# Moving the transposed quarter of a two-dimensional Haar transform from the forward to the inverse side of a long convolution kernel

## The chip, the core and the metric

The kernel runs on one core of one Trainium2 chip. The metric is the device time of one execution in microseconds (us); smaller is better. TensorE is called PE here, VectorE DVE, ScalarE ACT, GpSimd POOL and SyncE SP.

## What is computed

The input `x` is (4, 64, 256, 256) f32: four images in each of 64 channels. Four layers follow one another. Layers 0, 2 and 3 are long convolutions, whose filters come from a small sine network and factor into a filter over rows times one over columns for each channel:

```python
k = einsum('ijk,imk->ijmk', hx, hy)      # hx, hy: (256, 64), from the network
y = irfft2(rfft2(x, (512, 512)) * rfft2(k, (512, 512)) / 512)[:256, :256]
out = y + x * bias
```

Layer 1 works in the two-dimensional Haar domain (H rows and W columns, 8 levels each) and mixes channels, in P = 2 paths:

```python
f1 = haar2d(x)
for i in range(2):
    f3 = v[i] * f1
    f4 = einsum('bchw,oc->bohw', f3, conv_w[i])
    acc += sign(f4) * relu(abs(f4) - tau[i])
out = haar2d(acc, inverse=True) + x
```

(with the scales of the levels moved into `v`, `tau` and per-row factors, and with the last addition done as `+ f1` in the Haar domain).

## The kernel before

A convolution over one axis is a product with a 256x256 Toeplitz matrix. An image is two blocks of 128 partitions by 256 columns, the Toeplitz matrix has a triangular zero block, and so one axis of one image costs two matmuls of 256 and two of 128 columns (`toeplitz`, L228). The output comes out transposed, so that rows and then columns give the image back. One Haar direction is done along the free axis by GpSimd, level by level with additions and subtractions (`forward_free` L235, `inverse_free` L257). The other lies across partitions and takes TensorE: either 128x128 matmuls with a Haar matrix, or transposes into PSUM and the levels on another engine.

The four images of a channel are split into two groups (batches 0-1 and 2-3). A **round** handles M = 4 images: two channels of one group. Each group has 32 rounds in each of the phases A and C.

- **Phase A** (L295): the first convolution (`rows` L309, `columns` L316), then the Haar transform (`forward_free`, `product` L333), and a store of the coefficients to DRAM (`coef`, L427). A round is 12 pieces: four rows, four columns, four products of the round before. ACT copies the rows' result out of PSUM (L314); DVE adds the bias term and writes the columns' result (L325); ACT scales the product into `f` (L354).
- **Phase B** (L472): 64 steps of two units for each group: load all channels at some coefficient rows, mix the channels on PE (`mix`, L508), multiply by `v` on DVE (L512), sign and magnitude on ACT (L516, L519), subtract `tau` and threshold on DVE (L523, L526), add on POOL (L531, L534), and store to `mixed` (L547). A unit is three pieces; two PSUM tiles `f4` are in turn.
- **Phase C** (L580): load `mixed`, undo the free direction on POOL (L273, L275), undo the other, then the layers 2 and 3, each as rows and columns, and store `out`. A round of group 0 is 20 pieces, four of them `product` (L613); a round of group 1 is 16, and its inverse transform is done by transposes (`transposes` L624) with the levels on DVE (`inverse_halves` L642), in two halves q of two images each.

All engine orders are written out by hand. The stages lie, in time, as: A of group 0 alone, with the filter network of layers 2 and 3, the spreading of filters over DRAM and the scaling of `tau` interleaved as side pieces (`rest`, L191 to L195); A of group 1 beside B of group 0; C of group 0 beside B of group 1; C of group 1 alone. `beside` (L776) spreads the side pieces evenly over the main pieces. What evacuates PSUM is put off by `later` (L282) and issued at the start of the next piece by `flush`. PSUM tiles of phases A and C come from one pool of four banks (`bank`, L98), used in turn, so the bank of a piece is wanted again four pieces later. All DMAs are issued by SP in program order.

In phase A of group 0, rounds 0 to 29 (`paired`, L300) use matmuls for two of the four images. The other two go by eight transposes (`transposes`, L356), four scalings on ACT (L371, L372), and 17 DVE steps (`forward_psum`, L377), spread two to a piece over the next round; there the store of the round waits for piece 8 instead of piece 6 (L449 to L453). To make this possible the W coefficients stand in the same permuted order as the H coefficients: two halves of 128, each a Haar set of its own but for the coarsest pair. That pair is combined in `coarsest` (L418) for one direction and, for the other, in phase B's `store` when row 0 is stored (L539 to L546), with the two-column constant `first`. Phase C's `product` then is two independent 128-point inverse transforms per image: four 128x128 matmuls with `haarW`, and one ACT copy of 128x512 (L622).

Of the kernel before, what the change touches and what calls it, by code (L numbers as in the profile page):

```python
# [39 lines left out]
P = 128  # L41
# [12 lines left out]
M = CI * NB  # L54
# [15 lines left out]
def conv_haar_kernel(  # L70
    ctx: ExitStack, tc: tile.TileContext, x, zT, w1, wbd, cols, decay, bias, haarW, haarH, ident, wcol, wrow, mixT, first, v, tau, out
# [41 lines left out]
    tp = pool("t", 1, early)  # L113
    tps = pool("tps", 1, early, space=PSUM)
# [89 lines left out]
    wcol_sb = const.tile([P, 6], F32, tag="wcol", name="wcol_sb")  # L204
# [5 lines left out]

    first_sb = const.tile([P, 2], F32, tag="first", name="first_sb")
    nc.sync.dma_start(first_sb, first)
# [22 lines left out]
    def forward_free(src, dst, name):  # L235


        cur, half = src, HALF
        split = lambda t: t.rearrange("p n (h m) -> p n h m", h=2)
        while half >= 1:  # L240
            pair = cur.rearrange("p n (t q) -> p n t q", q=2)
            even, odd = pair[:, :, :, 0], pair[:, :, :, 1]
            if half == 1:
                nc.gpsimd.tensor_tensor(dst[:, :, 0:1], even, odd, ALU.add)
                yield
                nc.gpsimd.tensor_tensor(dst[:, :, HALF : HALF + 1], even, odd, ALU.subtract)
            else:
                m = half // 2
                at = dst.rearrange("p n (h q) -> p n h q", h=2)[:, :, :, m : 2 * m]
                nc.gpsimd.tensor_tensor(at, split(even), split(odd), ALU.subtract)  # L250
                yield
                cur = ac.tile([P, 2 * M, half], F32, tag=f"h{half}", name=f"{name}{half}", bufs=1)
                nc.gpsimd.tensor_tensor(cur, even, odd, ALU.add)
            yield
            half //= 2

    def inverse_free(src, dst, name):  # L257

# [27 lines left out]
    def flush():  # L286
        for op in waiting:
            op()
        waiting.clear()
# [5 lines left out]
    def phase_a():  # L295
# [3 lines left out]

        paired = ROUNDS - 2  # L300
# [32 lines left out]
        def product(t, j):  # L333
# [4 lines left out]
            if t < paired and j >= 2:  # L338
                if j == 2:
                    transposes(t)  # L340
                return
# [14 lines left out]
        def transposes(t):  # L356
            s = st[t]
            ps = tps.tile([P, 4, N], F32, tag="ps", name=f"tps_{t}")
            for e in range(2):
                for m in range(2):  # L360
                    for k in range(2):
                        data = s["fw"][:, 2 * (2 + e) + k, bass.ts(m, P)]
                        nc.tensor.transpose(ps[:, 2 * e + m, bass.ts(k, P)], data, ident_sb)
            odds = tp.tile([P, 4, HALF], F32, tag="odds", name=f"odds_{t}")
            pair = ps.rearrange("p n (t q) -> p n t q", q=2)

            def scale():
                for m in range(2):
                    by = wcol_sb[:, 4 + m : 5 + m]
                    every = pair.rearrange("p (e m) t q -> p e m t q", m=2)[:, :, m]  # L370
                    nc.scalar.activation(odds.rearrange("p (e m) t -> p e m t", m=2)[:, :, m], every[:, :, :, 1], AF.Copy, scale=by)  # L371
                    nc.scalar.activation(every[:, :, :, 0], every[:, :, :, 0], AF.Copy, scale=by)  # L372

            later(scale)
            s["pair"] = forward_psum(pair, odds, s["f"][:, 4:8], f"t{t}_")

        def forward_psum(pair, odds, dst, name):  # L377

            halves = dst.rearrange("p n (h q) -> p n h q", h=2)
            split = lambda t: t.rearrange("p n (h m) -> p n h m", h=2)
            even = pair[:, :, :, 0]
            d = halves[:, :, :, 64:128]
            nc.vector.tensor_tensor(d, split(even), split(odds), ALU.subtract)
            yield

            even2 = pair[:, :, :64, 1]
            odd2 = tp.tile([P, 4, 64], F32, tag="odd2", name=f"{name}odd")
            for q, o in enumerate((even2, odd2)):  # L390
                ds = d.rearrange("p n h (t q) -> p n h t q", q=2)[:, :, :, :, q]
                es = even.rearrange("p n (h t q) -> p n h t q", h=2, q=2)[:, :, :, :, q]
                nc.vector.scalar_tensor_tensor(split(o), ds, -0.5, es, ALU.mult, ALU.add)
                yield
            d = halves[:, :, :, 32:64]
            nc.vector.tensor_tensor(d, split(even2), split(odd2), ALU.subtract)
            yield
            cur = tp.tile([P, 4, 64], F32, tag="h64", name=f"{name}64")
            nc.vector.scalar_tensor_tensor(split(cur), d, -0.5, split(even2), ALU.mult, ALU.add)
            yield  # L400
            half = 32
            while half > 1:
                m = half // 2
                both = cur.rearrange("p n (t q) -> p n t q", q=2)
                d = halves[:, :, :, m : 2 * m]
                nc.vector.tensor_tensor(d, split(both[:, :, :, 0]), split(both[:, :, :, 1]), ALU.subtract)
                yield
                cur = tp.tile([P, 4, half], F32, tag=f"h{half}", name=f"{name}{half}")
                nc.vector.scalar_tensor_tensor(split(cur), d, -0.5, split(both[:, :, :, 0]), ALU.mult, ALU.add)
                yield  # L410
                half = m
            even, odd = cur[:, :, 0:1], cur[:, :, 1:2]
            nc.vector.tensor_tensor(dst[:, :, 0:1], even, odd, ALU.add)
            yield
            nc.vector.tensor_tensor(dst[:, :, HALF : HALF + 1], even, odd, ALU.subtract)
            yield

        def coarsest(t):  # L418

            by_product = 4 if t < paired else 2 * M  # L420
            pairs = st[t]["f"][:, :by_product].rearrange("p n (h q) -> p n h q", h=2)[:, :, :, 0]
            sd = ac.tile([P, 2 * M, 2], F32, tag="sd", name=f"sd_{t}", bufs=2)[:, :by_product]
            nc.gpsimd.tensor_tensor(sd[:, :, 0], pairs[:, :, 0], pairs[:, :, 1], ALU.add)
            nc.gpsimd.tensor_tensor(sd[:, :, 1], pairs[:, :, 0], pairs[:, :, 1], ALU.subtract)
            nc.gpsimd.tensor_copy(pairs, sd)
# [8 lines left out]
        def piece(t, j):  # L434
# [10 lines left out]
            elif j < 2 * M:  # L445
# [3 lines left out]
                if j == M + 2 and t > 1 + paired:  # L449
                    store(t - 2)  # L450
            else:
                if j == 2 * M and 1 < t <= 1 + paired:
                    store(t - 2)  # L453
# [4 lines left out]
            if j == 3 * M - 1 and 0 < t <= paired:  # L458
                run(st[t - 1]["pair"], 2)
            if j < 2 * M and 1 < t <= 1 + paired:  # L460
                run(st[t - 2]["pair"], 2)
# [10 lines left out]
    def phase_b(grp):  # L472
# [63 lines left out]
        def store(s):  # L536
            r0 = s * ROWS
            gt = st[s]["g"]
            if r0 == 0:  # L539

                top, low = (gt[:, 0].rearrange("p b (h k) -> p b h k", h=2)[:, :, h, :] for h in range(2))
                d = bp.tile([P, NB, N], F32, tag="sd", name=f"sd_{grp}", bufs=1)
                one, sign_ = first_sb[:, 0:1], first_sb[:, 1:2]
                nc.vector.tensor_scalar(d, top, one, None, ALU.mult)
                nc.vector.scalar_tensor_tensor(top, low, one, top, ALU.mult, ALU.add)
                nc.vector.scalar_tensor_tensor(low, low, sign_, d, ALU.mult, ALU.add)  # L546
# [33 lines left out]
    def phase_c():  # L580
# [32 lines left out]
        def product(t, n):  # L613
            s = st[t]
            ps = bank(f"c1ps{n}_{t}")
            for m in range(2):
                for h in range(2):
                    nc.tensor.matmul(  # L618
                        ps[:, m, bass.ts(h, P)], s["ci"][:, 2 * n + h, bass.ts(m, P)], haarW_sb, start=True, stop=True
                    )  # L620
            y = s["y", n] = image("t0", f"cz{n}_{t}")
            later(lambda: nc.scalar.copy(y, ps))  # L622

        def transposes(t, q):  # L624
# [15 lines left out]
            s["wops", q] = inverse_halves(ps, z, f"w{q}_{t}_")  # L640

        def inverse_halves(ps, dst, name):  # L642
            src = ps.rearrange("p n h q -> p (n h) q")
            cur, half = wp.tile([P, 8, 1], F32, tag="w1", name=f"{name}1", bufs=2), 1
            nc.vector.tensor_copy(cur, src[:, :, 0:1])
            yield
            while half < P:
                if half < P // 2:
                    o = wp.tile([P, 8, 2 * half], F32, tag=f"w{2 * half}", name=f"{name}{2 * half}", bufs=2)
                else:  # L650
                    o = dst.rearrange("p n (h q) -> p (n h) q", h=2)
# [49 lines left out]
        def piece(t, j):  # L701
# [25 lines left out]
            else:  # L727
# [10 lines left out]
                if j >= M + 8:  # L738
                    turn(alone, 1, 2)

        def piece_alone(t, j):
# [14 lines left out]
            if 3 <= j < 11:  # L756
                turn(t + 1, 0, 2)
            if j >= 8:
# [153 lines left out]
```

## Time and profile before

| what | us |
|---|---|
| median of 4 runs | 2961.3 (2953.39 to 2961.41) |
| profiled execution | 2957.78 |
| its span | 2956.0 |
| group-0 phase A | from about 35 to 498 |
| A of group 1 beside B of group 0 | to about 1200 |
| C of group 0 beside B of group 1 | to about 2210 |
| C of group 1 alone | to the end |

The profile's first part gives the busy time of each engine. Stages are told apart with a view that cuts the span into windows and gives, for each, the busy time of each engine, the granted TensorE clock and the DMA share. In a timeline, rows are: start, length, engine, line, operation, `output<-inputs`, shapes, count, and in brackets the idle time of the engine before the row, with what ended it. f32 matmuls are recorded as two instructions, transposes as one. The length of a PE row overlaps that of the next, so the pace of PE is read from starts.

### The profile page before, as it was taken

The page shows a single profiled execution, that of the slowest core. Times are in us where ns is not written, and L with a number is a line of the kernel's source. Part 1 is how long each engine was busy: PE and PEld are TensorE (multiplying, and loading weights), DVE is VectorE, ACT ScalarE, POOL GpSimd, SP SyncE. Part 2 cuts the span into 40 slices and gives each one's busy share as a digit, 9 for nine tenths or more (in the row PEclk, how much of TensorE's full clock was granted, in tenths as well). Part 3 has the DMA queues.
Part 4 walks back from the last instruction along what each step waited for, and adds up shares of the span by engine and source line. Part 5 has one row for each costly group of instructions (what it writes and reads, how often), then busy time and mean ns, then how long its engine had stood idle before and what let it go on. Part 6 is the DMA issues. An engine that isn't in the chain of part 4 may idle for free.

```text
span 2956.0 us, 47128 instructions
## 1 busy us (share of the span) xinstructions
PE 2865.5 (97%) x16680; PEld 2443.7 (83%) x16680; DVE 1873.9 (63%) x3065; ACT 1164.6 (39%) x1731; POOL 1967.6 (67%) x2500
## 2 busy tenths in 40 slices
PE   5999998999999999899999999999999999999999
PEld 5988998677777777878888888888899999999998
DVE  3666653788778887276666666666636655565555
ACT  1434443555555555344444444444432121212121
POOL 2766776788888888666666666766685445544550
PEclk9999999999999999999999999999999999999999
DMA  7956997898999997676686677667654454445442
GB/s 162 238 170 189 238 237 228 288 334 300 338 329 318 322 328 244 215 262 235 223 280 233 230 256 254 240 226 274 207 161 132 132 148 145 133 133 151 141 132 79
DMA packets 372145, 656.79 MB, mean 222 GB/s; under 512 B 33798, under 2 KB 273319, under 8 KB 371912
## 3 DMA queue, kind: packets, MB, share of 16 engines
q1 hardware_dynamic: 371912, 653.79, 69.0%
q8 instruction: 134, 2.20, 0.3%
q14 instruction: 99, 0.81, 0.1%
HBM read 438.24 MB, written 215.42 MB: 221 GB/s over the span
## 4 chain that ended last, share of the span: by engine, by line
PE 78%; DVE 6%; POOL 3%; issue 2%; DMA 2%; ACT 1%; SPq 0%; POOLq 0%; DVEq 0%; ACTq 0%
PE f L508 13%; PE c1c L232 8%; PE c2r L232 7%; PE c1r L232 7%; PE c2c L232 7%; PE a1ps L232 4%; PE c1c L233 4%; PE c2r L233 4%; PE c1r L233 4%; PE a2ps L232 4%; PE c2c L233 4%; PE c1ps L618 4%; PE a3ps L345 2%; PE a1ps L233 2%; DVE f L512 2%
## 5 line engine op out<-in xcount | busy, mean ns | idle before, releaser
L508 PE MATMUL f<-ft,mix_sb 128*128 128x512 f32 x1024 | 492.0, 603 | 30.0 <-DVE m L526 25.1
L516 ACT ACTIVATE m<-f 128x1024 f32<-128x1024 f32 x256 | 262.4, 1025 | 648.3 <-DVE f L512 623.2
L523 DVE TENSOR_TENSOR f<-f,tau 128x1024 f32<-128x1024 f32 x256 | 315.0, 1230 | 213.9 <-ACT f L519 213.9
L531 POOL TENSOR_TENSOR m<-m,ft 128x1024 f32<-128x1024 f32 x128 | 301.8, 2358 | 189.8 <-DVE m L526 189.3
L534 POOL TENSOR_TENSOR gt<-m,m 128x1024 f32<-128x1024 f32 x128 | 302.6, 2364 | 177.5 <-DVE m L526 117.0
L512 DVE TENSOR_TENSOR f<-f,v 128x1024 f32<-128x1024 f32 x256 | 314.5, 1229 | 111.1 <-PE f L508 109.4
L232 PE MATMUL a1ps<-toep,x 128*128 128x256 f32 x1024 | 307.7, 383 | 16.7 <-DMA toep<-filt 16.7
L232 PE MATMUL a2ps<-toep,ay 128*128 128x256 f32 x1024 | 310.4, 385 | 11.0 <-ACT ay L314 11.0
L526 DVE SCALAR_TENSOR_TENSOR m<-f,m 128x1024 f32<-128x1024 f32 x256 | 311.0, 1215 | 0.1
L508 PEld LDWEIGHTS f<-ft,mix_sb 128*128 128x128 f32 x1024 | 175.6, 191 | 163.3 <-issue 123.5
L232 PE MATMUL c2r<-toep,cy 128*128 128x256 f32 x1024 | 305.8, 380 | 0.0
L232 PE MATMUL c1c<-toep,ch 128*128 128x256 f32 x1024 | 305.8, 380 | 0.0
L232 PE MATMUL c2c<-toep,ch 128*128 128x256 f32 x1024 | 305.8, 380 | 0.0
L670 ACT COPY ch<-c2r 128x512 f32<-128x512 f32 x256 | 148.5, 588 | 381.7 <-PE c2r L233 381.5
L670 ACT COPY ch<-c1r 128x512 f32<-128x512 f32 x256 | 149.5, 590 | 333.6 <-PE c1r L233 332.7
L684 DVE SCALAR_TENSOR_TENSOR o<-cy,bias_sb,c2c 128x512 f32<-128x512 f32 x256 | 188.4, 742 | 144.8 <-PE c2c L233 144.7
L519 ACT ACTIVATE f<-f 128x1024 f32<-128x1024 f32 x256 | 263.5, 1029 | 0.0
L325 DVE SCALAR_TENSOR_TENSOR x<-x,bias_sb,a2ps 128x512 f32<-128x512 f32 x256 | 188.1, 743 | 102.4 <-PE a2ps L233 57.8
L250 POOL TENSOR_TENSOR fw<-x 128x1024 f32<-128x1024 f32 x64 | 121.2, 1894 | 161.0 <-DVE x L325 161.0
L273 POOL TENSOR_TENSOR i<-i,g 128x16 f32<-128x16 f32 (+5 forms) x384 | 208.8, 544 | 27.2
L273 POOL TENSOR_TENSOR i<-g 128x8 f32<-128x8 f32 x64 | 14.2, 222 | 315.0 <-DMA g<-mixed 315.0
L354 ACT ACTIVATE f<-a3ps,wcol_sb 128x512 f32<-128x512 f32 x196 | 131.3, 685 | 226.9 <-PE a3ps L345 139.7
(87 smaller groups left out, 6472.9 us busy)
## 6 DMA issues: line engine op xcount, KB each, us to landing
toep<-filt SPq DMA_DIRECT2D x768, 128.0 KB, 3.4
x<-in_x SPq DMA_DIRECT2D x256, 256.0 KB, 6.1
coef<-f SPq DMA_DIRECT2D x128, 512.0 KB, 4.8
ft<-coef SPq DMA_DIRECT2D x128, 512.0 KB, 7.1
v<-in_v SPq DMA_DIRECT2D x128, 512.0 KB, 7.2
tau<-taus SPq DMA_DIRECT2D x128, 512.0 KB, 7.0
mixed<-gt SPq DMA_DIRECT2D x128, 512.0 KB, 5.9
g<-mixed SPq DMA_DIRECT2D x128, 512.0 KB, 5.5
```

Of the source, the lines that this page charges most:

```text
L232: nc.tensor.matmul(ps[:, m, :], data[:, 0, cut], t[:, which, :], start=True, stop=False)
L233: nc.tensor.matmul(ps[:, m, HALF:], data[:, 1, cut], t[:, which, :HALF], start=False, stop=True)
L273: nc.gpsimd.tensor_tensor(even, s, d, ALU.add)
L508: nc.tensor.matmul(un[u]["f4"][:, j, :], mix_sb[:, u % 2, :], f[:, j, :], start=True, stop=True)
L512: nc.vector.tensor_tensor(f4, f4, weights(st[u // 2]["v"], u % 2), ALU.mult)
L516: nc.scalar.activation(un[u]["m"], un[u]["f4"], AF.Sign)
L519: nc.scalar.activation(un[u]["f4"], un[u]["f4"], AF.Abs)
L523: nc.vector.tensor_tensor(f4, f4, weights(st[u // 2]["tau"], u % 2), ALU.subtract)
L526: nc.vector.scalar_tensor_tensor(un[u]["m"], un[u]["f4"], 0.0, un[u]["m"], ALU.max, ALU.mult)
L531: nc.gpsimd.tensor_tensor(m0, m0, data(st[s]["f"]), ALU.add)
L534: nc.gpsimd.tensor_tensor(data(st[s]["g"]), m0, un[2 * s + 1]["m"], ALU.add)
L670: later(lambda: nc.scalar.copy(y, ps))
```

## The change

The transposes go out of phase A and into phase C's product, and the W coefficients return to natural order.

- Phase A of group 0: all rounds use matmuls for all four images, as rounds 30 and 31 and group 1 did. `transposes`, `forward_psum` and their pools are gone; every store stands at piece 6.
- `forward_free` writes each level's differences as one contiguous run, and phase B's `store` has no repair of row 0; `first` is gone. The constants for `v`, `tau` and the per-row scales follow the natural order.
- Phase C of group 0: per image, the coarse 128 coefficients take two matmuls with `haarW`, the finest 128 two transposes with the identity. ACT copies the coarse half out of PSUM (128x256) one piece later, and another piece later two DVE operations form the last level into `cz`, reading the transposed half in PSUM.
- Phase C of group 1: the levels on DVE run over one chain of 256 instead of two of 128 side by side, 17 steps instead of 15 for each half q, and may start the second half one piece earlier and end the first one piece later.
- `flush` empties its list before it runs it, so that an operation may put off another.

```diff
     def forward_free(src, dst, name):
...
-                m = half // 2
-                at = dst.rearrange("p n (h q) -> p n h q", h=2)[:, :, :, m : 2 * m]
-                nc.gpsimd.tensor_tensor(at, split(even), split(odd), ALU.subtract)
-                yield
+            nc.gpsimd.tensor_tensor(dst[:, :, half : 2 * half], even, odd, ALU.subtract)
+            yield
+            cur = dst[:, :, 0:1]
+            if half > 1:
                 cur = ac.tile([P, 2 * M, half], F32, tag=f"h{half}", name=f"{name}{half}", bufs=1)
-                nc.gpsimd.tensor_tensor(cur, even, odd, ALU.add)
+            nc.gpsimd.tensor_tensor(cur, even, odd, ALU.add)
...
-            if t < paired and j >= 2:
-                if j == 2:
-                    transposes(t)
-                return
             ps = bank(f"a3ps{j}_{t}")
...
-                if j == M + 2 and t > 1 + paired:
+                if j == M + 2 and t > 1:
                     store(t - 2)
             else:
-                if j == 2 * M and 1 < t <= 1 + paired:
-                    store(t - 2)
...
-            if j == 3 * M - 1 and 0 < t <= paired:
-                run(st[t - 1]["pair"], 2)
-            if j < 2 * M and 1 < t <= 1 + paired:
-                run(st[t - 2]["pair"], 2)
...
         def store(s):
-            if r0 == 0:
-
-                top, low = (gt[:, 0].rearrange("p b (h k) -> p b h k", h=2)[:, :, h, :] for h in range(2))
-                d = bp.tile([P, NB, N], F32, tag="sd", name=f"sd_{grp}", bufs=1)
-                one, sign_ = first_sb[:, 0:1], first_sb[:, 1:2]
-                nc.vector.tensor_scalar(d, top, one, None, ALU.mult)
-                nc.vector.scalar_tensor_tensor(top, low, one, top, ALU.mult, ALU.add)
-                nc.vector.scalar_tensor_tensor(low, low, sign_, d, ALU.mult, ALU.add)
...
         def product(t, n):
             s = st[t]
-            ps = bank(f"c1ps{n}_{t}")
+
+            ps = bank(f"c1ps{n}_{t}").rearrange("p w (m q) -> p w m q", m=2)
             for m in range(2):
-                for h in range(2):
-                    nc.tensor.matmul(
-                        ps[:, m, bass.ts(h, P)], s["ci"][:, 2 * n + h, bass.ts(m, P)], haarW_sb, start=True, stop=True
-                    )
+                cut = bass.ts(m, P)
+                nc.tensor.matmul(ps[:, 0, m], s["ci"][:, 2 * n, cut], haarW_sb, start=True, stop=True)
+                nc.tensor.transpose(ps[:, 1, m], s["ci"][:, 2 * n + 1, cut], ident_sb)
             y = s["y", n] = image("t0", f"cz{n}_{t}")
-            later(lambda: nc.scalar.copy(y, ps))
+            half = ac.tile([P, 2, P], F32, tag="half", name=f"half{n}_{t}", bufs=2)
+            pair = y.rearrange("p m (t q) -> p m t q", q=2)
+
+            def finest():
+                nc.vector.tensor_tensor(pair[:, :, :, 0], ps[:, 1], half, ALU.add)
+                nc.vector.tensor_tensor(pair[:, :, :, 1], half, ps[:, 1], ALU.subtract)
+
+            later(lambda: (nc.scalar.copy(half, ps[:, 0]), later(finest)))
...
-            while half < P:
-                if half < P // 2:
-                    o = wp.tile([P, 8, 2 * half], F32, tag=f"w{2 * half}", name=f"{name}{2 * half}", bufs=2)
-                else:
-                    o = dst.rearrange("p n (h q) -> p (n h) q", h=2)
+            while half < N:
+                o = dst
+                if half < HALF:
+                    o = wp.tile([P, 4, 2 * half], F32, tag=f"w{2 * half}", name=f"{name}{2 * half}", bufs=2)
...
-            if 3 <= j < 11:
+            if 3 <= j < 12:
                 turn(t + 1, 0, 2)
-            if j >= 8:
+            if j >= 7:
                 turn(t + 1, 1, 2)
```

More of the change, by code (lines that the diff above doesn't have):

```diff
@@ L70, in conv_haar_kernel @@
 def conv_haar_kernel(
-    ctx: ExitStack, tc: tile.TileContext, x, zT, w1, wbd, cols, decay, bias, haarW, haarH, ident, wcol, wrow, mixT, first, v, tau, out
+    ctx: ExitStack, tc: tile.TileContext, x, zT, w1, wbd, cols, decay, bias, haarW, haarH, ident, wcol, wrow, mixT, v, tau, out
 ):
@@ L112, in conv_haar_kernel @@
     mps = early.enter_context(tc.tile_pool(name="mlp_ps", bufs=2, space=PSUM))
-    tp = pool("t", 1, early)
-    tps = pool("tps", 1, early, space=PSUM)
     def constant(name, src, shape):
@@ L202, in conv_haar_kernel @@
     nc.sync.dma_start(haarH_sb, haarH)
-    wcol_sb = const.tile([P, 6], F32, tag="wcol", name="wcol_sb")
+    wcol_sb = const.tile([P, 4], F32, tag="wcol", name="wcol_sb")
     nc.sync.dma_start(wcol_sb, wcol)
@@ L209, in conv_haar_kernel @@
     nc.sync.dma_start(mix_sb, mixT)
-    first_sb = const.tile([P, 2], F32, tag="first", name="first_sb")
-    nc.sync.dma_start(first_sb, first)
     def load_toeplitz(l, t, bufs):
@@ L238, in forward_free @@
         cur, half = src, HALF
-        split = lambda t: t.rearrange("p n (h m) -> p n h m", h=2)
         while half >= 1:
@@ L242, in forward_free @@
             even, odd = pair[:, :, :, 0], pair[:, :, :, 1]
-            if half == 1:
-                nc.gpsimd.tensor_tensor(dst[:, :, 0:1], even, odd, ALU.add)
-                yield
-                nc.gpsimd.tensor_tensor(dst[:, :, HALF : HALF + 1], even, odd, ALU.subtract)
-            else:
-                m = half // 2
-                at = dst.rearrange("p n (h q) -> p n h q", h=2)[:, :, :, m : 2 * m]
-                nc.gpsimd.tensor_tensor(at, split(even), split(odd), ALU.subtract)
-                yield
+            nc.gpsimd.tensor_tensor(dst[:, :, half : 2 * half], even, odd, ALU.subtract)
+            yield
+            cur = dst[:, :, 0:1]
+            if half > 1:
                 cur = ac.tile([P, 2 * M, half], F32, tag=f"h{half}", name=f"{name}{half}", bufs=1)
-                nc.gpsimd.tensor_tensor(cur, even, odd, ALU.add)
+            nc.gpsimd.tensor_tensor(cur, even, odd, ALU.add)
             yield
@@ L286, in flush @@
     def flush():
-        for op in waiting:
+        ops = list(waiting)
+        waiting.clear()
+        for op in ops:
             op()
-        waiting.clear()
     def run(ops, count):
@@ L298, in phase_a @@
         total = GROUPS * ROUNDS
-        paired = ROUNDS - 2
         st = [dict() for _ in range(total + 1)]
@@ L354, in product @@
             later(lambda: nc.scalar.activation(dst, ps, AF.Copy, scale=wcol_sb[:, m : m + 1]))
[L356 to L416, printed above, removed]
@@ L418, in coarsest @@
         def coarsest(t):
-            by_product = 4 if t < paired else 2 * M
-            pairs = st[t]["f"][:, :by_product].rearrange("p n (h q) -> p n h q", h=2)[:, :, :, 0]
-            sd = ac.tile([P, 2 * M, 2], F32, tag="sd", name=f"sd_{t}", bufs=2)[:, :by_product]
+            pairs = st[t]["f"].rearrange("p n (h q) -> p n h q", h=2)[:, :, :, 0]
+            sd = ac.tile([P, 2 * M, 2], F32, tag="sd", name=f"sd_{t}", bufs=2)
             nc.gpsimd.tensor_tensor(sd[:, :, 0], pairs[:, :, 0], pairs[:, :, 1], ALU.add)
@@ L639, in transposes, with inverse_psum @@
                 s["y", 2 * q + e] = z[:, 2 * e : 2 * e + 2]
[L640 to L644, printed above, removed]
+            s["wops", q] = inverse_psum(ps.rearrange("p n h q -> p n (h q)"), z, f"w{q}_{t}_")
+        def inverse_psum(src, dst, name):
+            cur, half = wp.tile([P, 4, 1], F32, tag="w1", name=f"{name}1", bufs=2), 1
             nc.vector.tensor_copy(cur, src[:, :, 0:1])
             yield
-            while half < P:
-                if half < P // 2:
-                    o = wp.tile([P, 8, 2 * half], F32, tag=f"w{2 * half}", name=f"{name}{2 * half}", bufs=2)
-                else:
-                    o = dst.rearrange("p n (h q) -> p (n h) q", h=2)
+            while half < N:
+                o = dst
+                if half < HALF:
+                    o = wp.tile([P, 4, 2 * half], F32, tag=f"w{2 * half}", name=f"{name}{2 * half}", bufs=2)
                 pair = o.rearrange("p n (t q) -> p n t q", q=2)
@@ L737, in piece @@
                     turn(alone, 0, 2)
-                if j >= M + 8:
+                if j >= M + 7:
                     turn(alone, 1, 2)
@@ L853 @@
     w = np.abs(full).max(axis=1)
-    v, tau = (
-        a[f"L1_conv_{n}"].reshape(2, N, N).transpose(0, 2, 1)[:, order][:, :, order] for n in ("v", "tau")
-    )
+    v, tau = (a[f"L1_conv_{n}"].reshape(2, N, N).transpose(0, 2, 1)[:, :, order] for n in ("v", "tau"))
     by_row = lambda t: f(t.reshape(2, 2, P, N).transpose(2, 0, 1, 3))
@@ L866 @@
         mix[:, g, :, :, g] = a["L1_conv_conv_w"].transpose(2, 0, 1)
-    odd = np.arange(P) % 2
     arrays = {
@@ L894 @@
         "ident": np.eye(P, dtype=np.float32),
-        "wcol": f(np.concatenate([(w**2)[order].reshape(2, P).T, w[order].reshape(2, P).T, (w**2)[order].reshape(2, P).T / 2], axis=1).astype(np.float32)),
+        "wcol": f(np.concatenate([(w**2).reshape(2, P).T, w.reshape(2, P).T], axis=1).astype(np.float32)),
         "wrow": f(w[order].astype(np.float32)),
         "mixT": f(mix.reshape(P, 2, P)),
-        "first": f(np.stack([1.0 - odd, 2.0 * odd - 1.0], axis=1).astype(np.float32)),
         "v": by_row(v),
```

## The prediction

> **What bounds the kernel now.** I read the busy table of the page first, then stages cut by the windows view, then single instructions in the timeline.
>
> ```profile
> PE 2865.5 (97%) x16680; PEld 2443.7 (83%) x16680; DVE 1873.9 (63%) x3065; ACT 1164.6 (39%) x1731; POOL 1967.6 (67%) x2500
> ```
>
> TensorE (PE) is the bound. The windows view (start:end, length, busy time of PE, PEld, DVE, ACT, POOL, granted clock, DMA share, GB/s) shows where it is gapless:
>
> ```profile
> 264.00:449.00 185.00, 185.00 (x1242) 173.34 (x1242) 113.38 (x297) 76.43 (x140) 141.10 (x266) 1.00 0.93 240
> 900.00:1100.00 200.00, 193.80 (x978) 145.48 (x979) 160.32 (x153) 114.16 (x149) 178.46 (x207) 1.00 0.93 318
> 1345.00:1990.00 645.00, 645.00 (x3570) 526.86 (x3569) 426.52 (x430) 298.06 (x422) 435.32 (x409) 1.00 0.71 245
> 2210.00:2900.00 690.00, 690.00 (x4378) 640.09 (x4378) 404.26 (x1157) 141.96 (x243) 341.20 (x481) 1.00 0.47 137
> ```
>
> Row 1 is phase A of group 0 (call it A0), row 3 phase C of group 0 beside phase B of group 1 (C0), row 4 the last phase C (C1): PE never idle, clock full. Row 2, A of group 1 beside B of group 0, has VectorE (DVE) 80% busy and PE 3% idle. So a change in A0 or C0 is worth its PE time, plus the idle gaps it opens or closes.
>
> **PE in A0: +27.3 us.** Timeline of one A0 round, PE rows (start, length, line, operation, count):
>
> ```profile
> 277.61 1.95 PE L345 MATMUL a3ps<-haarH_sb,fw 128*128 128x128 f32 x16
> 279.40 1.04 PE L363 MATMUL tps<-ident_sb,fw 128*128 128x128 f32 x8
> 280.27 0.60 PE L232 MATMUL a1ps<-toep,x 128*128 128x256 f32 x2
> ```
>
> Starts tell the pace, since lengths overlap. An f32 matmul is two instructions, and 16 of them take 279.40-277.61 = 1.79, so 0.224 per matmul; a transpose is one instruction, and eight take 0.87, so 0.109 each. Thirty rounds get 8 matmuls for 8 transposes: 8 x 0.115 = 0.91 a round. The period confirms it: 13.14 us with transposes (264.47, 277.61, 290.75), 14.05 with the full product (a3ps at 1170.77, 1184.82, 1198.87). 30 x 0.91 = +27.3.
>
> **PE in C0: -29.3 us.** Each of 128 images has four L618 matmuls (32 passes in 3.57 us, 0.223 a matmul); two become transposes: 256 x 0.1145 = -29.3. Here the two kinds alternate, which the trace never shows. Between blocks of them (279.40, 280.27) no gap is seen, so I take none; the bound above is 0.11 on each of the 256, as if a transpose cost a matmul (+29).
>
> The Trainium skill, TensorE: Matmul & The Clock Gate, Part 4, speaks against this: transposes do not count as activity for the clock gate, so a stretch of them may fall to half rate. This trace disagrees at this density: rows 1 and 4 hold 8 per 13 us and 16 per 25 us at clock 1.00. By the page, a halved clock for one product stretch of 2.7 us in each of 32 rounds would be an estimated +85 us.
>
> **The W order: -7 us.** Natural order drops the first-row repair in phase B's store (L544-L546, twice). DVE and PE rows of the timeline, first time:
>
> ```profile
> 543.34 1.56 DVE L544 TENSOR_SCALAR sd<-gt,first_sb 128x512 f32<-128x512 f32 x1
> 544.93 2.72 DVE L545 SCALAR_TENSOR_TENSOR gt<-gt,first_sb 128x512 f32<-128x512 f32 x1
> 547.69 1.41 DVE L546 SCALAR_TENSOR_TENSOR gt<-gt,first_sb,sd 128x512 f32<-128x512 f32 x1
> 552.55 3.38 PE L508 MATMUL f<-ft,mix_sb 128*128 128x512 f32 x4 [3.58 <-DVE m L526]
> ```
>
> The threshold of the next unit stands behind them; PE idles 3.58, then runs the four passes in 3.38 where 1.72 is usual: 5.2 lost. The second time (1271-1284) it idles 1.1 twice and loses 0.6: 2.8. Total 8; I take -7, since DVE may be late by itself (0 to -12, all of the DVE work removed). On GpSimd (POOL) the permuted write goes: L250 (permuted) 1894 ns, L253 (plain) 1893: nothing.
>
> **A0's DVE and queues: -12 us.** The 17 DVE steps per round and four scalings on ScalarE (ACT, 2 x (473+448) = 1.84) go; two more L354 come (2 x 0.685 = 1.37). ACT and DVE were not the bound, but DVE holds up PE at two places.
>
> (a) The filter network's three layers sit in rounds of 18.86, 19.89 and 21.21 instead of 13.14: 20.5 extra, of which 3 x 0.87 is their own matmuls; 17.9 is waiting (11.0 idle, the rest slow clock). Its sine waits in ACT's queue for DVE's chain, and phase A's copies stand behind it:
>
> ```profile
> 195.98 0.70 PE L232 MATMUL a2ps<-toep,ay 128*128 128x256 f32 x2 [3.96 <-ACT ay L314]
> ```
>
> The chain (4.6 us) started 1.2 and some 2 us late behind pair steps in two layers, 0.2 in the third. About 3.5 of 11.0 idle goes, times 17.9/11.0: -6 (0 to -12).
>
> (b) Near 475 tau is awaited on DVE, and the columns' evacuation stands behind it:
>
> ```profile
> 474.52 1.22 DVE L180 TENSOR_TENSOR tau_sb<-tau_sb,wrow_sb 128x1024 f32<-128x1024 f32 x1 [5.18 <-DMA tau_sb<-in_tau]
> 480.57 5.31 PE L345 MATMUL a3ps<-haarH_sb,fw 128*128 128x128 f32 x32 [5.70 <-DVE t L409]
> ```
>
> PE loses 5.7 idle and 5.31-3.57 = 1.7 slow: 7.4. Between tau and the first evacuation (476.6 to 479.7) lie 3.1 us of pair steps, which go. SyncE's (SP) store of coef moves from piece 8 to piece 6, past no other DMA but a filter spread or tau where one falls there, and no longer waits for DVE; two longer rounds give tau's load 1.8 us more. -6 (0 to -7.4). Elsewhere the earlier store only frees a buffer sooner.
>
> **What C0 pays: +12 us.** Before, `cz` came by one ACT copy (0.59) one piece after the product. Now ACT copies a half (nearest rows, 128x256, 448 to 473 ns), and another piece later DVE makes two 128x256 operations (nearest rows L654 and L656, 425 and 417): 0.84 an image, 3.4 a round. DVE goes from 66% to about 77%. The PSUM bank is freed by DVE too, and phase C's rows wait for `cz` four pieces after its product. In the queue ahead of it can stand a unit's multiply and threshold (1.13 each by their starts), behind a mix that PE must finish. Say mix ends at t: threshold done t+2.26, first `cz` t+3.1. PE meanwhile has three products (3 x 0.665, t+2.0), a wait of 1.1; all four, t+2.66, 0.4. With the column evacuation (0.65) ahead and the sign before the half copy on ACT, about 1.4. Laying phase B's pieces against the products by the program order: 3 rounds of 1.1, 4 of 1.4, 2 of 0.7, 7 of 0.4, the rest free: 13, taken as 12. Bounds: 0 (DVE catches up), and 1.4 in all 32 rounds, +45. A 1.1 us wait at 1283.38 left the next four passes at 1.98, so these do not cost clock. Phase B's own chain keeps cover: a mix follows the threshold it needs by about 6.9 us of program, against 3.5 of DVE work. The `half` buffers (2) let ACT wait for DVE; ACT is 46% busy there.
>
> **Rest: +1.** Around 1208 PE waits for POOL anyway, so the first round's 0.9 gain is lost. In C1 each half image chain gets two more DVE steps (about 0.16 each by L656's 128x8 form, 153): 21 us of DVE, hidden under a gapless PE with DVE at 59%; it starts a piece earlier and ends in the same piece. Uncovered it would be +21.
>
> Sum: +27.3 -29.3 -7 -6 -6 +12 +1 = **-8 us**. The profiled execution took 2957.78 (span 2956.0 and 1.8 around it), so 2949.8; the median of the runs is 2961.3, from which it is 2953.3. I give **2951**.
>
> **Rivals.**
> 1. *DVE becomes C0's bound (slower).* Place: DVE's queue at the first four rows pieces; price 0.85 to 1.4 us a round. From 0.85 (26 us in all) the sum passes +6; at 1.25 in each of 32 rounds (40) it is +20: 2971 to 2974. For it: the 80%-busy row above has 3% PE idle, which over some 900 us is 27. Against: in that row a unit comes each 4.9 us, in C0 each 6.9. 20%.
> 2. *C0 hides the finest level wholly.* Then -20: 2938. For it: 645 of 645 us busy now, DVE at 66%. 17%.
> 3. *The early gaps stay.* The network's chain and tau's load are late by DMA and POOL (DMA share 0.93), not by pair steps: +12 undone, +4: 2962. PE's swap alone nets -2, so the change then does next to nothing. 23%.
> Forecast: 40%.
>
> The measurement tells about 0.2% (6 us) from nothing. The forecast's 40% lies mostly beyond it (35 faster, 5 same), rival 2 faster, rival 3 same, rival 1 slower with a little same: faster 0.52, same 0.29, slower 0.19. The range 2932 to 2974 runs from rival 2 with more of the early gaps closed, to rival 1's upper price; steady alternation cost, C1 uncovered and a falling clock are left out.
>
> **What would show it.** A0 round period 14.05; C0 c1ps alternating at 0.665 per image with no gap; waits of PE on `cz` of some 12 us; no PE idle near 549, 1277 and 475; the network rounds' waits near 12 rather than 18; DVE near 77% in C0. It is wrong if alternation is slower than 0.112 per pass, if PE waits on `cz` in nearly every round, or if the granted clock falls below 1.00 in C0.

## The result, and the profile after

| | before | after |
|---|---|---|
| median of the runs, us | 2958.58 (60 runs) | 2963.49 (42 runs) |
| span of the profiled execution, us | 2956.0 | 2961.6 |
| mean granted clock over the span | 0.993 | 0.996 |

The ratio is 1.0016, with a 95% interval of 1.0012 to 1.0021: the changed kernel is about 5 us slower, which is clear of noise but less than the 0.2% that the prediction called no change. The forecast was 8 us faster. The two profiled spans differ by 5.6 us, so the stages of the two traces can be set against each other.

The busy table of the changed kernel:

```profile
PE 2864.2 (97%) x16664; PEld 2440.3 (82%) x16664; DVE 1811.7 (61%) x2933; ACT 1129.8 (38%) x1671; POOL 1967.8 (66%) x2500
```

PE's work is the same as before to 1.3 us: A0 got what C0 lost. The stages, cut by the windows view as before (start:end, length, busy time of PE, PEld, DVE, ACT, POOL, clock, DMA share, GB/s):

```profile
264.00:449.00 185.00, 185.00 (x1264) 174.11 (x1263) 38.87 (x52) 67.16 (x107) 131.70 (x249) 1.00 0.87 219
900.00:1100.00 200.00, 192.65 (x981) 144.35 (x980) 162.16 (x156) 113.70 (x148) 175.35 (x195) 1.00 0.94 320
1345.00:1990.00 645.00, 632.71 (x3410) 510.24 (x3409) 478.91 (x590) 283.23 (x421) 439.12 (x411) 1.00 0.72 245
2215.00:2900.00 685.00, 685.00 (x4345) 635.40 (x4344) 413.27 (x1265) 142.01 (x242) 344.74 (x482) 1.00 0.47 139
```

Row 1 (A0) is still gapless, with a third of the DVE work. Row 4 (C1) is still gapless. Row 3 (C0) is not: 645.00 of 645 busy before, 632.71 now, at a clock of 1.00. The table of PE's waits (line, what it waited for, us in total, times, longest) says on what:

```profile
PE f L424 <- DVE m L442: 22.0, 37, 1.5
...
PE c1r L228 <- DVE cz L535: 8.1, 8, 1.2
...
PE c1r L228 <- ACT half L537: 5.0, 6, 1.2
...
PE a1ps L228 <- ACT f L339: 4.5, 1, 4.5
PE a2ps L228 <- ACT ay L303: 4.5, 2, 2.8
...
PE c1r L228 <- ACT ch L584: 4.1, 3, 1.4
```

`c1r`, the rows of phase C's first convolution, never waited before; now it waits 17 times, for 17.2 us of listed idle time.

Following one instruction of the same round through both traces gives the account by stage. The lag is the start after less the start before.

| where | lag, us | what happened since the row above |
|---|---|---|
| first mix of B, 516.67 and 532.31 | +15.6 | A0 |
| a3ps, 1170.77 and 1181.13 | +10.4 | first repair gap gone, -5.3 |
| first c1r of C0's second round, 1248.98 and 1260.35 | +11.4 | PE waits for POOL here |
| start of the next round, 1285.20 and 1293.49 | +8.3 | second repair gap, -2.2, and 0.9 of PE |
| start of C1, 2227.09 and 2232.82 | +5.7 | 30 rounds of C0 |
| end | +5.6 | C1 |

From 1249 on C0 gains 5.6 us. Its PE work is shorter by 27.5 there and the second repair is 2.2, so **24 us** were lost to new waits. The same 24 come out by adding, round by round, what each round's period has over the period before less 0.92.

### The profile page after: what moved, and what is told of

Read it like the earlier page. It is cut to its first block, busy times and chain, and to the rows that moved or that the text cites. A ratio compares the mean times of both kernels' runs of the same rounds, so it can differ in the third digit from the quotient of the medians.

```text
span 2961.6 us, 46832 instructions
## 1 busy us (share of the span) xinstructions
PE 2864.2 (97%) x16664; PEld 2440.3 (82%) x16664; DVE 1811.7 (61%) x2933; ACT 1129.8 (38%) x1671; POOL 1967.8 (66%) x2500
## 4 chain that ended last, share of the span: by engine, by line
PE 76%; DVE 7%; issue 3%; ACT 2%; DMA 2%; POOL 2%; SPq 0%; ACTq 0%; POOLq 0%; DVEq 0%
PE f L424 11%; PE c1c L228 8%; PE c2r L228 7%; PE c2c L228 7%; PE c1r L228 7%; PE a1ps L228 5%; PE a2ps L228 4%; PE c1c L229 4%; PE c2r L229 4%; PE c2c L229 4%; PE a3ps L330 4%; PE c1r L229 3%; DVE f L428 3%; PE a1ps L229 2%; PE a2ps L229 2%
## 5 line engine op out<-in xcount | busy, mean ns | idle before, releaser
L330 PEld LDWEIGHTS a3ps<-haarH_sb,fw 128*128 128x128 f32 x2048 | 241.9, 193 | 26.4 <-issue 20.4
L339 ACT ACTIVATE f<-a3ps,wcol_sb 128x512 f32<-128x512 f32 x256 | 173.0, 686 | 224.7 <-PE a3ps L330 203.5
L330 PE MATMUL a3ps<-haarH_sb,fw 128*128 128x128 f32 x2048 | 247.1, 276 | 4.8 <-POOL fw L242 4.8
```

What stands on the lines that cost most here:

```text
L330: nc.tensor.matmul(ps[:, e, bass.ts(k, P)], s["fw"][:, 2 * (n + e) + k, bass.ts(m, P)], haarH_sb[:, k, :], start=True, stop=True,)
```

## The experiments

**Theory W** says that the two halves of the change are worth what PE's counts say (+27.3 in A0, -29.3 in C0, some -7 for the W order), and that C0's rows wait some 24 us for `cz`, because the half copy and the last level stand behind phase B's pieces on ACT and DVE. The rivals are that alternation of transposes and matmuls costs PE time, that A0 costs more than its matmuls, or that DVE is too full in C0 whatever the order.

### The two halves apart

e1 is the kernel before with no round by transposes in A0:

```diff
-        paired = ROUNDS - 2
+        paired = 0
```

> The kernel before with only phase A of group 0 changed: all rounds use the full product and store at piece 6, nothing else. Theory T (the change is two independent parts that add): +15 to +16 us on before, the shift that the traces show at the end of phase A, ratio 1.0053; near 475 no PE idle. Rival R (the early gaps close only together with the W part): +27, the bare price of the matmuls, ratio 1.009.

Measured: 2971.46 us, ratio 1.0052 (1.0039 to 1.0064), or +15.4 us, and some 12 to 19 by the interval. This is what the traces give for A0 (+15.6), and it excludes the rival's +27.

e2 is the changed kernel with A0's transposes and pair steps put back, over W in natural order:

```diff
+        paired = ROUNDS - 2
...
+            if t < paired and j >= 2:
+                if j == 2:
+                    transposes(t)
+                return
```

> The kernel after with phase A's transposed pairs put back, so natural W order and the new product in phase C alone. Theory T: -10 us on before (-5 and -3 from the dropped repair, -28 PE, +24 waits at cz, +1 at the change of phases), ratio 0.9966, and the same 17 or so PE waits before c1r as after. Rival R: parts that do not add, near 0 or above.

Measured: 2948.87 us, ratio 0.9972 (0.9963 to 0.9981), or -8.3. Its waits of `c1r` are those of the changed kernel to the tenth of a us. So the halves add, within their intervals, and C0's part with the W order is a gain of only 8 where PE's count and the repair alone would give some 36.

### What C0's waits are worth

e3 leaves the last level out; ACT copies both halves, as before the change:

```diff
-            later(lambda: (nc.scalar.copy(half, ps[:, 0]), later(finest)))
+            later(lambda: nc.scalar.copy(y.rearrange("p m (h q) -> p h m q", h=2), ps))
```

> The kernel after, leaving out the last Haar level of the first group's phase C on VectorE: ScalarE copies both PSUM halves into cz as they are, one piece after the product; TensorE's work is unchanged. Theory W (the waits at cz are the loss): PE does not wait before c1r, -23 us on after, about -18 on before (0.994). Rival P (alternating matmuls and transposes or the clock is slower than the starts say): no gain on after, +5 on before.

Measured: 2939.07 us, ratio 0.9939 (0.9926 to 0.9951): 24 under the changed kernel, and no wait of `c1r` at all. PE's alternation is unchanged in e3, so it isn't what costs.

e4 leaves DVE its two operations, but they need no copy by ACT; they read `ci` in its place, so the coarse half stays untransformed:

```diff
-            half = ac.tile([P, 2, P], F32, tag="half", name=f"half{n}_{t}", bufs=2)
+            half = s["ci"][:, 2 * n].rearrange("p (m q) -> p m q", m=2)
...
-            later(lambda: (nc.scalar.copy(half, ps[:, 0]), later(finest)))
+            later(lambda: later(finest))
```

> The kernel after, with the coarse half not copied by ScalarE: VectorE's two operations take the untransformed coarse coefficients from SBUF in its place, so the coarse half of the inverse W transform is left out of the result; their place in the queue is unchanged. If the ScalarE hop (a copy queued behind phase B's sign, which waits for VectorE) makes the waits: -12 to -20 on after. If VectorE's own queue makes them: -0 to -6 on after. I expect about half, -10.

Measured: 2956.53 us, ratio 0.9996 (0.9986 to 1.0005), 7 under the changed kernel by the medians and 5 by the profiled spans (2961.6 and 2956.7), instead of the 10 expected. So the hop over ACT is some 5 to 7 of the 24, and the rest remains with `cz` coming from DVE alone:

```profile
PE c1r L228 <- DVE cz L535: 4.3, 8, 0.9
...
PE c1r L228 <- issue: 3.5, 3, 1.2
...
PE c1r L228 <- ACT ch L584: 2.5, 3, 0.8
PE c1r L228 <- PE c1ps L528: 1.5, 3, 0.5
```

The rows "issue" and "PE" name no releaser that ended just before the wait did. At each of these six waits DVE's L535 ended 0.10 us before PE started, so I read them with the first. All 17 waits of the changed kernel are still there, but those of a round's third image fall from at most 1.37 us to 0.82, and those of the fourth from at most 1.18 to 0.22.

### Is it DVE's load, or the place of the pieces?

e5 changes no instruction. Phase B's pieces are not issued after a round's last columns piece and its first three products; they are caught up one a piece afterwards:

```diff
-    def beside(main, side, lead, tail):
+    def beside(main, side, lead, tail, held=()):
...
             want = len(side) * max(0, k + 1 - lead) // max(1, len(main) - lead - tail)
+            if held and k < len(main) - 1:
+                want = done if p in held else min(want, done + 1)
...
-    beside(main[: -10 * M], phase_b(1), 5 * M, 0)
+    held = [c[t * 5 * M + j] for t in range(1, ROUNDS) for j in (-1, 0, 1, 2)]
+    beside(main[: -10 * M], phase_b(1), 5 * M, 0, held)
```

> The kernel after, with phase B's side pieces in phase C of group 0 not issued after the last columns and the first three products, and caught up one a piece later. Same instructions on every engine. Theory W (the last Haar level stands behind phase B's multiply, sign and threshold): no PE wait before c1r, -18 to -23 on after, about -15 on before (0.995). Rival L (the three engines' hand-over PE, ScalarE, VectorE, PE is too long by itself): waits stay, 0 to -6 on after. Rival M (phase B bunched makes PE wait for the threshold instead): waits before f, near 0.

Measured: 2940.01 us, ratio 0.9941 (0.9928 to 0.9953), 23 under the changed kernel. C0 by the windows view of e5, beside row 3 above:

```profile
1345.00:1990.00 645.00, 645.00 (x3507) 523.32 (x3506) 493.65 (x609) 292.41 (x434) 446.66 (x424) 1.00 0.74 252
```

DVE is busier than in the changed kernel (493.65 of 645, 77%, against 74%), and PE has no gap. The load of DVE was not the cause; the place of phase B's pieces in the program was. In the changed kernel a multiply and a threshold of phase B stand directly ahead of 33 of the 128 images' operations in DVE's queue, and PE waits at 17 of them; in e5 they stand ahead of 19, and PE waits at none. This settles theory W against the third rival. PE's waits on the threshold (`f` on `m`) also come down a little, from 22.0 us to 20.6.

e6 is e2 and e5 together: transposes in A0 and in C0, natural order, held pieces.

> e2_pairs_natural with the same delay of phase B's side pieces. If the parts add: -9 - 20 = about -29 on before, ratio 0.990, the fastest so far. If the delay only shifts waits: -9.

Measured: 2925.28 us, ratio 0.9891 (0.9877 to 0.9904), 33 under the kernel before.

### The W order by itself

e8 is the kernel before without the three operations on row 0:

```diff
-            if r0 == 0:
...
-                nc.vector.tensor_scalar(d, top, one, None, ALU.mult)
-                nc.vector.scalar_tensor_tensor(top, low, one, top, ALU.mult, ALU.add)
-                nc.vector.scalar_tensor_tensor(low, low, sign_, d, ALU.mult, ALU.add)
```

> The kernel before, leaving out only the repair of row 0 in phase B's store, which combines the coarsest pair of W. Theory: the two PE gaps near 549 and 1277 go, -8 on before, ratio 0.9973. Rival (VectorE is late there by itself): -2 or less.

Measured: 2951.26 us, ratio 0.9975 (0.9966 to 0.9984), or -7, as the two repairs make in the traces (5.3 and 2.2).

### The early gaps

The prediction laid a part of the network's gaps to DVE's pair steps. With the pair steps gone they were still 18.3 us of longer rounds out of 21.4. Theory S: ACT's queue stands behind a sine that waits for DVE's range reduction, whatever else DVE does. e7 takes the sine out of the layer's piece and makes it a piece of its own among the side pieces (on e6):

```diff
-            st["h"] = part("h", bufs=2)
-            nc.scalar.activation(st["h"], u, AF.Sin)
+            st["u"] = u
+
+        def sine():
+            st["h"] = part("h", bufs=2)
+            nc.scalar.activation(st["h"], st["u"], AF.Sin)
...
-        return [lambda d=d: layer(d) for d in range(3)] + [last]
+        return [op for d in range(3) for op in (lambda d=d: layer(d), sine)] + [last]
```

> e6 with each sine of the filter network for layers 2 and 3 issued as a side piece of its own, some 18 pieces after its VectorE chain. Theory S (the three early gaps, 17.9 us of waiting, come from the sine queued on ScalarE ahead of phase A's copies while VectorE works on its input): 13 to 18 us less than e6. Rival V (VectorE's own chain holds up the columns' evacuation): the gaps stay, 0 to -5.

Measured: 2921.62 us, ratio 0.9879 (0.9866 to 0.9893): 3.7 under e6, not 13 to 18, and as the two ratios' intervals overlap, it isn't shown to be faster than e6 at all. The network's gaps did go (some 13.7 us in that stretch), but 20 side pieces where there were 17 also moved the filter spreads, and two new waits and a longer round behind tau gave it back: in the profiled executions the first mix of B comes at 515.98 in e7 and at 514.84 in e6. From the timeline of e7, PE rows:

```profile
419.59 1.22 PE L233 MATMUL a1ps<-toep,x 128*128 128x256 f32 x2 [5.27 <-ACT f L349]
...
463.67 1.16 PE L233 MATMUL a1ps<-toep,x 128*128 128x256 f32 x2 [2.83 <-ACT f L349]
```

e9 therefore leaves every side piece in its place, and issues the sine eight main pieces after its layer (on e6):

```diff
-            st["h"] = part("h", bufs=2)
-            nc.scalar.activation(st["h"], u, AF.Sin)
+            def sine():
+                st["h"] = part("h", bufs=2)
+                nc.scalar.activation(st["h"], u, AF.Sin)
+
+            soon.append([8, sine]) if n == 2 else sine()
...
         for k, p in enumerate(main):
             p()
+            tick()
```

(`tick` counts the entries of `soon` down and runs one that reaches zero.)

> The kernel of e6_pairs_natural_hold with the sine of each later layer of the small network issued eight main pieces after its layer, so that the sine waits on ScalarE's queue for nothing, and with every side piece at the place that it had in e6 (e7 put three more pieces among them and shifted the filter spreads). Theory S, the network's gaps are ScalarE's queue standing behind a sine that waits for VectorE: the gaps of the network's rounds (about 13 us in e6) go and nothing comes back near 420 and 464 us; 2912 us, ratio to before about 0.985. Rival: the product of the network's layer holds its bank longer with the late sine, or the later rounds give the time back: ratio 0.988 to 0.989, as e7 and e6.

Measured: 2910.54 us, ratio 0.9838 (0.9823 to 0.9854), 14.7 under e6 by the medians and 9.0 by the profiled spans (2919.9 and 2910.9; e6's profiled execution was the fastest of its four). The rows `a2ps <- ACT ay` (11.0 us in e6) are gone from the waits. One wait got longer: the gap on tau is 6.59 us where e6 has 4.54. DVE waits as long for tau's load in both (5.37 and 5.49), so the reason is not shown.

e10 moves that scaling to the fifth place among the side pieces (on e9):

```diff
-    rest.append(scale_tau)
+    rest.insert(4, scale_tau)
```

> As e9_sine_delayed, and the scaling by tau is moved to the fifth place among the side pieces, so that the pieces behind it shift by one place. Before's gap near 475 us (5.7 us idle and 1.7 us at a lower clock) stands behind that scaling, and with the paired columns put back it stands in e6 and e9 too. If it is the place of the scaling alone: 6 us off e9, about 2906 us, ratio 0.983. Rival: the early loads or the shifted spreads make a wait in its place: e9's time or up to 5 us more.

Measured: 2907.35 us, ratio 0.9824 (0.9809 to 0.984). The timelines of e9 and of e10, PE's rows of the product in those rounds:

```profile
446.97 1.95 PE L349 MATMUL a3ps<-haarH_sb,fw 128*128 128x128 f32 x16
467.91 5.93 PE L349 MATMUL a3ps<-haarH_sb,fw 128*128 128x128 f32 x32 [6.59 <-DVE t L413]
484.16 3.74 PE L349 MATMUL a3ps<-haarH_sb,fw 128*128 128x128 f32 x32
```

```profile
450.46 1.95 PE L349 MATMUL a3ps<-haarH_sb,fw 128*128 128x128 f32 x16
463.60 3.74 PE L349 MATMUL a3ps<-haarH_sb,fw 128*128 128x128 f32 x32
477.65 3.74 PE L349 MATMUL a3ps<-haarH_sb,fw 128*128 128x128 f32 x32
```

The gap on tau at 467.91 is gone (PE now waits 1.83 at 167.06, where the scaling stands in e10), the first mix of B comes 6.0 us sooner (498.45 against 504.45), and the profiled span is 7.7 shorter. The medians differ by only 3.2, and the two ratios' intervals overlap, so how much of the 6 us the move itself is worth stays open. e10 is the fastest version here, 51 us under the kernel before: both halves of the kernel use transposes, W is in natural order, and three sets of pieces stand elsewhere in the program.

## Why the prediction was wrong

The terms of the sum beside what the two traces show:

| step of the prediction | forecast | measured |
|---|---|---|
| PE in A0 | +27.3 | +27.3 |
| (a) the network's rounds | -6 | -3.1 |
| (b) tau | -6 | -7.4 |
| first mix of B (no term) | 0 | -1.2 |
| the W order | -7 | -5.3 and -2.2 |
| PE in C0 | -29.3 | -29.3 |
| what C0 pays | +12 | +24 |
| rest | +1 | +2.9 |
| sum | -8 | +5.6 |

The rest is what is left of the stretch around 1208 to 1250, where PE waits for POOL and the first rounds' gain is lost.

**The step that failed is "What C0 pays: +12 us": it measured +24.** Those 12 us are most of the 13.6 between the two sums. The mechanism, `cz` standing behind phase B's multiply and threshold, was right and its size was not. The durations were not too short: the two DVE operations took 418 and 412 ns (forecast 425 and 417), and the copy 373 (forecast 448 to 473). What was wrong was the place where the delay was looked for. The prediction laid phase B's pieces against each round's *first* image: sixteen rounds with a wait there, 13 us together. In the trace the first image waits six times, 5.0 us; the second image four times (3.4 us), the third three times (4.1) and the fourth four times (4.7). So the term was too high for the first image, and those 12.2 us of the others had none. Each image's `cz` is a step of its own in DVE's queue, and a unit of phase B that is issued amid the products puts its multiply and threshold ahead of whichever image comes next. The timeline of the changed kernel around the longest of these waits (rows of DVE, ACT and PE):

```profile
1513.20 0.37 ACT L537 COPY half<-c1ps 128x256 f32<-128x256 f32 x1 [0.63 <-PE f L424]
...
1514.14 0.41 DVE L534 TENSOR_TENSOR cz<-c1ps,half 128x256 f32<-128x256 f32 x1
...
1514.47 0.41 DVE L535 TENSOR_TENSOR cz<-half,c1ps 128x256 f32<-128x256 f32 x1
...
1514.80 1.23 DVE L428 TENSOR_TENSOR f<-f,v 128x1024 f32<-128x1024 f32 x1
...
1515.94 1.22 DVE L442 SCALAR_TENSOR_TENSOR m<-f,m 128x1024 f32<-128x1024 f32 x1
...
1516.19 0.38 PE L229 MATMUL c1r<-toep,cz 128*128 128x128 f32 x2
...
1517.07 0.41 DVE L534 TENSOR_TENSOR cz<-c1ps,half 128x256 f32<-128x256 f32 x1
...
1517.40 0.41 DVE L535 TENSOR_TENSOR cz<-half,c1ps 128x256 f32<-128x256 f32 x1
...
1517.95 0.70 PE L228 MATMUL c1r<-toep,cz 128*128 128x256 f32 x2 [1.37 <-ACT ch L584]
```

Read it upward from the last row, the rows piece of the third image. PE had finished the second image's at 1516.41 (two passes of 0.11 from 1516.19). The third image's `cz` was complete when L535 ended at 1517.81, 0.14 before PE started; the trace puts the wait down to the copy `ch`, which ended 0.09 later, but this image does not read it. Its half lay ready from 1513.57 on. DVE had written the second image's `cz` at 1514.88, and then took a multiply and a threshold of phase B, which put the third back by 2.27 us (1514.80 to 1517.07). It is the same pair, t+2.26, that the prediction set ahead of the first image alone. At all 17 waits this pair, back to back, is what DVE does directly before the waiting image's two operations. The wait of the fourth image at 1906.55 has the same two operations ahead of it (1903.40 and 1904.53), its half copied at 1901.80.

ACT's queue is the smaller share: DVE sat idle 18.6 us, in 23 places, until a half copy came, and taking the copy away (e4) gave 5 to 7 of the 24.

A part of the error, too, is that a wait costs more than its listed idle time. The last pass before it is recorded with 0.27, which reaches 0.16 beyond its pace of 0.11. At 1517.95 PE starts 1.54 after it could have, with 1.37 listed, and at 1417.87 it is 0.67 with 0.50 listed:

```profile
1417.87 0.67 PE L228 MATMUL c1r<-toep,cz 128*128 128x256 f32 x2 [0.50 <-ACT half L537]
1418.37 0.39 PE L229 MATMUL c1r<-toep,cz 128*128 128x128 f32 x2
```

The passes after the wait take 0.50 to the next row, where 0.43 is usual. Read in this way, the 17 waits and three new ones on the mix have 18.5 us listed, cost 21.7 by the starts, and 1.5 more in the passes behind them: 23.2 of the 24. The prediction took the passes behind such a wait as free, from the one at 1283.38; by the starts there (1283.38 and 1285.20) they took 1.82, where 1.72 is usual.

**What was right.** Alternation costs PE nothing. Timeline of PE, two of the four images of a product in C0:

```profile
1414.55 0.38 PE L527 MATMUL c1ps<-haarW_sb,ci 128*128 128x128 f32 x2
1414.77 0.27 PE L528 MATMUL c1ps<-ident_sb,ci 128*128 128x128 f32 x1
1414.88 0.39 PE L527 MATMUL c1ps<-haarW_sb,ci 128*128 128x128 f32 x2
1415.10 0.27 PE L528 MATMUL c1ps<-ident_sb,ci 128*128 128x128 f32 x1
1415.21 0.39 PE L527 MATMUL c1ps<-haarW_sb,ci 128*128 128x128 f32 x2
```

From 1414.55 to 1415.21, an image takes 0.66, at 0.22 a matmul and 0.11 a transpose, as forecast (0.665). The clock held 1.00 in row 3. The Trainium skill, TensorE: Matmul & The Clock Gate, Part 4, has a 128x128 bf16 transpose at about 275 ns in one kernel and says that the full clock does not engage for transposes. The recorded length of the f32 ones here, 0.27, is near that figure, but the next pass starts 0.11 later, and the clock did not fall: the measurement decides, and neither the estimated +85 us of a halved clock nor a price of 275 ns is seen. A0's rounds have the period 14.05, and PE has no gap where the repair stood. DVE came to 74% in C0 (about 77% forecast), C1 hid its extra steps, and tau's gap went whole, as (b)'s outer bound had it.

**(a) The network** gave half of the forecast. PE's first two waits on `ay` came down only from 2.54 and 3.96 to 1.70 and 2.77, and in the third layer the wait (4.52) only moved, to a rows piece that waits for ACT's scaling of a product (`f`):

```profile
171.62 0.70 PE L228 MATMUL a2ps<-toep,ay 128*128 128x256 f32 x2 [1.70 <-ACT ay L303]
...
201.00 0.70 PE L228 MATMUL a2ps<-toep,ay 128*128 128x256 f32 x2 [2.77 <-ACT ay L303]
...
233.83 1.22 PE L228 MATMUL a1ps<-toep,x 128*128 128x256 f32 x2 [4.55 <-ACT f L339]
```

e9 shows the cause: with the sine issued later, the waits on `ay` go though the pair steps are there; what is left in those three rounds are waits of 0.36, 0.76 and 1.36 on DVE.

**The rivals.** Rival 3 (+4 us, 2962) came closest in time, for another reason: it kept all the early gaps, but 10.5 us of them went; the loss was C0's. Rival 1 had the right place and nearly the right price (26 us in all where it starts, 24 measured), but took DVE's share to be the cause, which e5 excludes. Rival 2, C0 wholly hidden, is what e5 makes true by order alone: -18 against the kernel before, where -20 was forecast for it.

Two numbers of the prediction do not follow from its own rows. Rival 1's upper price, -20 and +40, makes +20, which is 2978 from the profiled execution and not 2971 to 2974, so the range ends below it. And the last phase C has its 16 transposes in a round of 22.7 us, not 25.

What stays open: why the waits fall where they do. With rounds counted from 0, the first image waits in the even rounds from 6 to 16, the third in 9, 11 and 13, the fourth in the odd rounds from 21 to 27, and the second in round 1 and in 24, 26 and 28. The order of the two lists against each other may explain it; the pattern was not predicted, and no run took one round apart.

## What to carry to other kernels

When a step goes from one engine to a chain of two, it takes a place in two queues, once for each instance. Lay the other stage's pieces against *every* instance in a round, not the first. Where PE is the bound and the other engines are at 75%, don't price a new step by its time or its engine's share: price it by what is ahead of it in program order, and try the order first, since it costs nothing (here 23 us for a few lines).

An early engine in a strict queue is worth as much as a fast one: putting off a waiting sine by eight pieces was worth 9 to 15 us here, but adding pieces to an evenly spread list moves all the others, so change one place at a time.

## What the runs showed of the hardware

- A transpose recorded as 0.27 us keeps PE for 0.11, alternating with f32 matmuls or in blocks; an f32 matmul of 128 columns keeps it for 0.22.
- A short wait of PE costs more than the idle time that is listed for it. Over the 20 waits in C0 it is 0.16 us each before the start (21.7 us against 18.5 listed) and 0.07 each in the passes behind.
- DVE reading one operand in PSUM and one in SBUF takes 412 to 418 ns for 128x256 f32, and ACT's copy of as much out of PSUM 373 ns, against 588 to 590 for 128x512: half the size costs 63% of the time.
- PE stayed gapless with DVE at 77% in e5, while the changed kernel lost 24 us over C0 with DVE at 74%.
